# Layer 3's gate and gcn products by pairs of tiles, with seven products of half chunks

## The chip, the cores and the metric

The kernel runs on one NeuronCore of a Trainium2 chip. The metric is the device time of one execution in microseconds. Engine names are those of the profile: PE is TensorE's matmul, PEld its load of the stationary operand, DVE VectorE, ACT ScalarE, POOL GpSimd, SP SyncE. Everything is fp32.

## The reference

Four graph layers on 2708 nodes with 512 features, each behind a layernorm and a relu and added to x:

```python
h = maximum(_layernorm(x), 0.0); x = x + L0(h, adj, weight)      # relu(norm(adj + I) @ h @ W)
h = maximum(_layernorm(x), 0.0); x = x + L1(h, adj, W, b)        # norm(adj) @ h @ W.T + b
h = maximum(_layernorm(x), 0.0); x = x + L2(h, adj, W)           # relu(norm(adj + I) @ h @ W)
h = maximum(_layernorm(x), 0.0); x = x + L3(h, adj, adj, ...)
```

Layer 3, which the change is about (adj_a and adj_b are both adj):

```python
type_sum = adj @ x                                               # here x is the h above
attn_a = sigmoid(concatenate([type_sum, x], axis=1) @ Wa.T + ba)
attn_b = sigmoid(concatenate([type_sum, x], axis=1) @ Wb.T + bb)
h = x @ W_sa
scores = (h @ a_sa[0, :512])[:, None] + (h @ a_sa[0, 512:])[None, :]
e = where(adj != 0, exp(-leaky_relu(scores, 0.01)), 0.0)
x_a = (e / (sum(e, axis=1, keepdims=True) + 1e-05)) @ h
x_b = adj @ (x @ W_gcnb) + b_gcnb
return sigmoid(attn_a * x_a + attn_b * x_b)
```

The kernel forms adj @ x once and multiplies that by W_gcnb (for x_b) and by the first halves of Wa and Wb (for the two gates).

## The kernel before, in words

The nodes lie in 20 full tiles of 128 rows (tile t belongs to quarter t // 5), tile 20 with 4 x 32 rows and tile 21 with 4 x 8. `h` holds the layer's input for all tiles. `agg` holds the transposed aggregate adj @ h: its indices are the feature half f, the node half i, the chunk c of a feature half, the quarter q of a node half, and the column. A chunk is 128 features, so a tile of `agg` is four blocks of 128 x 128 (f, c), which serve as stationary operands.

`aggregate` builds `agg` by an outer scheme of seven products (numbered 1 to 7, `outer_product`), each of which runs an inner scheme of seven (`inner_x`, `inner_y`, `multiply`), for each of two column parts u. The order is 1, 7, 2, 4, the tail rows of quarters 0 and 1, 6, `ends_of_sums` (L665, L666), 5, the tail rows of quarters 2 and 3 (`tails`, L603, L608, L653), then the epilogue of tiles 0 to 9 (H1), product 3, and the epilogue of tiles 10 to 21 (H2). Products 5 and 3 write node half 1 only.

In layer 3 the epilogue is `gated`. `wg_sb` holds the gcn weights and gate columns as [128, chunk, k, 257]: 256 columns of W_gcnb and one gate column for each k. For each tile `tile_product` (L203) makes two results of 257 columns in PSUM, each the sum over four chunks; ACT takes the tanh of the last column (L1052), DVE adds the bias row (L1061), ACT multiplies by the gate (L1062), and POOL's queue stores the result to `xbs` in DRAM (L1063). Results rotate through the two banks of `ps_out`. Five more banks, `ps_agg`, serve the aggregation and the attention's `pe`.

After the epilogue the attention runs in 40 steps: `e_step` loads a block of adj and scores it on ACT and DVE (L1131, L1135, L1136), PE multiplies it by `h` (L1214) into four banks `pe0` to `pe3`, DVE sums its columns (L1225). The first step is asked for inside the last epilogue. Finished tiles go through `attention`, which loads x and xbs through `xt_places` (L916).

`ends` is a hand-laid buffer: `w_place` (the layer's weights), `misc` (four rows of 512: score vectors in layer 3's aggregation, later the column sums), `xt_places` (rows of x on the way), `y_places` (two rows) and `bg_bc` (the bias row). `take` hands out places in turn.

The program's text gives each instruction its priority and its dependences; the framework's scheduler fixes the order on each engine before the run, and may put a later instruction that it holds to be ready in front of an earlier one. Each engine then takes its own list in order.

Of the kernel before, what the change touches and what calls it, by code (L numbers as in the profile page):

```python
# [8 lines left out]
FP = mybir.dt.float32  # L9
AF = mybir.ActivationFunctionType  # L10
ALU = mybir.AluOpType

P = 128
D = 512
NC = D // P
# [3 lines left out]
KT = Q // P  # L19
# [3 lines left out]
W = (Q + 1) // U  # L23
NF = NQ * KT
# [4 lines left out]
GT = 3  # L29
# [1 line left out]


NO = 7
ENDS = NC * D + 2 * NC + (4 + GT + 1 + 2 + 1) * D


@with_exitstack
def gnn_kernel(
# [20 lines left out]
    nc = tc.nc  # L59
# [5 lines left out]
    upool = ctx.enter_context(tc.tile_pool(name="upool", bufs=1))  # L65
# [3 lines left out]
    ps_agg = ctx.enter_context(tc.tile_pool(name="ps_agg", bufs=5, space=bass.MemoryType.PSUM))  # L69
    ps_out = ctx.enter_context(tc.tile_pool(name="ps_out", bufs=2, space=bass.MemoryType.PSUM))  # L70
# [24 lines left out]
    hd = const.tile([P, NT, 4], FP, name="hd")  # L95
    mv0 = const.tile([P, NT, 2], FP, name="mv0")
    ga = const.tile([P, NT, 2], FP, name="ga")
# [5 lines left out]
    xbs = [dram.tile([P, D], FP, name=f"xbs{t}") for t in range(NT)]  # L103
# [13 lines left out]
    agg = big.tile([P, 2, 2, 2, 2, U * W], FP, name="agg")  # L117
# [4 lines left out]
    obuf = big.tile([P, NO, BLK], FP, name="obuf")  # L122
    ends = big.tile([P, ENDS], FP, name="ends")

# [12 lines left out]
    w_place, ends_o = ends[:, 0 : NC * D + 2 * NC], NC * D + 2 * NC  # L137
    misc, ends_o = ends[:, ends_o : ends_o + 4 * D], ends_o + 4 * D
    xt_places = [ends[:, ends_o + k * D : ends_o + (k + 1) * D] for k in range(GT + 1)]
    ends_o += (GT + 1) * D  # L140
    y_places = [ends[:, ends_o + k * D : ends_o + (k + 1) * D] for k in range(2)]
    ends_o += 2 * D
    bg_bc = ends[:, ends_o : ends_o + D]
    assert ends_o + D == ENDS

    def take(places):

        places.append(places.pop(0))
        return places[-1]

    def new_y():
        return take(y_places)
# [6 lines left out]
    def full_cols(a, t):  # L159
        k = t % KT  # L160
        return a[:, k * P : (k + 1) * P]

    def repeat(g, n):

        while n < P:
            nc.vector.tensor_copy(g[..., n : 2 * n], g[..., 0:n])
            n *= 2

    def tile_cols(a, t, again=False):


        cs = [a[:, f, :, c] for f in range(a.shape[1]) for c in range(a.shape[3])]
        if t < NF:
            q = t // KT
            return [full_cols(c[:, q // 2, q % 2], t) for c in cs]
        o, m = (KT * P, R0) if t == NF else (KT * P + R0 - PAD, R1P)
        if a.shape[5] == R0 + R1:
            o -= KT * P
        g = new_y().rearrange("p (c n) -> p c n", c=NC)
        for c, src in enumerate(cs):  # L180
            nc.vector.tensor_copy(
                g[:, c, 0 : NQ * m].rearrange("p (i q r) -> p i q r", i=2, q=2),
                src[:, :, :, o : o + m],
            )
        n = NQ * m
        if again:
            repeat(g[:, 0 : len(cs)], n)
            n = P
        return [g[:, c, 0:n] for c in range(len(cs))]

    def tile_product(t, cs, ws):

        n = ws[0].shape[-1]

        def bank():
            return ps_out.tile([P, n], FP, tag="out", name="po")

        po = bank()  # L200
        if t <= NF:
            for c in range(NC):
                nc.tensor.matmul(po, cs[c], ws[c], start=(c == 0), stop=(c == NC - 1))  # L203
            return po
        for c in range(NC):
            nc.tensor.matmul(po[c * G : (c + 1) * G], cs[c], ws[c], start=True, stop=True)
        y = new_y()[:, 0:n]
        nc.scalar.copy(y, po)
        po = bank()
        nc.tensor.matmul(po, all_again, y, start=True, stop=True)  # L210
        return po
# [84 lines left out]

    left = ends[:, 4 * BLK : ENDS]
    acct = [
# [734 lines left out]
    GW = D // 2 + 1  # L1033
    wg_sb = w_place.rearrange("p (c k o) -> p c k o", c=NC, k=2)
    for k in range(2):
# [5 lines left out]
            wg_sb[:, :, k, D // 2 :], wab[0:D, k : k + 1].rearrange("(c p) o -> p c o", p=P)  # L1041
        )

    def gated(ts):

        for t in ts:
            cs = tile_cols(agg, t)
            po = []
            for k in range(2):
                pk = tile_product(t, cs, [wg_sb[:, c, k, :] for c in range(NC)])  # L1050

                nc.scalar.activation(  # L1052
                    ga[:, t, k : k + 1], pk[:, D // 2 :], AF.Tanh,
                    bias=hd[:, t, 2 + k : 3 + k], scale=0.5,
                )
                po.append(pk)
            nc.vector.tensor_scalar(ga[:, t, :], ga[:, t, :], 0.5, 0.5, ALU.mult, ALU.add)
            y = new_y()
            for k in range(2):
                f = slice(k * (D // 2), (k + 1) * (D // 2))  # L1060
                nc.vector.tensor_add(y[:, f], po[k][:, 0 : D // 2], bg_bc[:, f])  # L1061
            nc.scalar.activation(y, y, AF.Copy, scale=ga[:, t, 1:2])  # L1062
            nc.gpsimd.dma_start(xbs[t], y)  # L1063

    def again(ts, fs):

# [48 lines left out]
    def column_rows(q):  # L1115

        ra, rb = (
            spool.tile([P, U * W], FP, tag=f"s{1 + k + 2 * (q % 2)}", name=f"r{k}") for k in (0, 1)
        )
        for k, r in enumerate((ra, rb)):  # L1120
            nc.vector.memset(r[:, Q : U * W], 0.0)
            nc.gpsimd.dma_start(r[:, 0:Q], ab_rows[q, k, 0:Q].partition_broadcast(P))
        return ra, rb
# [14 lines left out]
    def place(t):  # L1138

        if t < NF:  # L1140
            o = (t // KT) * Q + (t % KT) * P
            return [(0, P, o)]
        if t == NF:
            return [(q * R0, R0, q * Q + KT * P) for q in range(NQ)]
        return [(q * R1P + PAD, R1, q * Q + KT * P + R0) for q in range(NQ)]
# [25 lines left out]
    def e_step(q, u, b):  # L1171

        cu = slice(u * W, (u + 1) * W)
        ra, rb = (a[:, cu] for a in lines[q])
        if b < NQ:
            blk = load_o("y11", b, q, u)
            ts = list(range(b * KT, (b + 1) * KT))
            scores(blk, ts, ra, rb)
            return [(t, blk[:, k, :]) for k, t in enumerate(ts)], [blk]
        tl = load_tails(q, u)  # L1180
        for s in range(2):
            scores(tl[:, s : s + 1, :], [NF + s], ra, rb)
        return tl, []
# [4 lines left out]
    def gated_and_ready(ts):  # L1188

        nonlocal ready  # L1190
        if ts[0] < half:
            return gated(ts)
        gated(ts[:4])
        lines[0] = column_rows(0)
        gated(ts[4:])
        ready = e_step(*steps[0])

    hooks[6] = row_scales
    hooks[3] = lambda: again(range(half, NF), slice(0, D // 2))
    aggregate(False, gated_and_ready, hooks)  # L1200
    wsa_sb = load_w(wsa)
    todo = []
    for n, (q, u, b) in enumerate(steps):
# [35 lines left out]
        elif todo:  # L1239
            t, se_t = todo.pop(0)  # L1240
# [70 lines left out]
```

## Time and profile before

| | us |
|---|---|
| median of 3 runs | 2091.28 (2090.2 to 2091.34) |
| profiled execution | 2089.36 |
| its span, first to last instruction | 2087.6 |
| its granted TensorE clock | 0.998 of full |
| gates' products, tiles 0 to 9 | 1490.1 to 1525.2 of the span |
| gates' products, tiles 10 to 21, among attention products | 1564.8 to 1624.3 |

The span is the profile's zero to end; the time is 1.76 us longer. A row of a group names source line, engine, operation, output<-input, shapes and count; then busy time and mean duration; then the idle time of the engine before these instructions and what ended it. On PE one fp32 matmul leaves two records, and the mean duration overlaps with its neighbours', so periods are taken from the timeline.

### The profile page before, as it was taken

The numbers are of one execution on the slowest core, as the hardware profiler recorded it, in microseconds if no ns is written. First come the engines' busy times: TensorE is split into PE (matmuls) and PEld (weight loads), VectorE is DVE, ScalarE is ACT, GpSimd is POOL, SyncE is SP. The second block draws the span as 40 slices with busy tenths as digits, with TensorE's granted clock in tenths as the row PEclk, the third lists the DMA queues.
The fourth block names the chain that finished last, engine by engine and source line by source line (L and its number), as shares of the span: only waits on it lengthen the run. The fifth ranks groups of instructions, "written<-read, shape, count | busy, mean of one in ns | idle before, by whom it ended". The sixth has DMA issues, their size and how long they took to land.

```text
span 2087.6 us, 19939 instructions
## 1 busy us (share of the span) xinstructions
PE 2044.6 (98%) x7286; PEld 1272.0 (61%) x7286; DVE 1397.4 (67%) x2427; ACT 404.5 (19%) x818; POOL 193.8 (9%) x350
## 2 busy tenths in 40 slices
PE   5999999999999999999999999999999999999998
PEld 2566655656666554666664556666777666666665
DVE  4678877666767777866686889868539355565512
ACT  1430001130000011100002120000119233444411
POOL 0111111120000012100002120001001001000011
PEclk9999999999999999999999999999999999999999
DMA  9998594554545354655444564545552333233220
GB/s 370 303 378 267 184 346 166 189 191 169 173 155 190 127 181 140 239 170 172 160 155 162 201 232 169 189 154 164 179 188 74 117 104 115 98 104 102 94 71 26
DMA packets 80770, 363.65 MB, mean 174 GB/s; under 512 B 11140, under 2 KB 16172, under 8 KB 80544
## 3 DMA queue, kind: packets, MB, share of 16 engines
q1 hardware_dynamic: 50672, 245.43, 34.0%
q0 software_dynamic: 30000, 116.95, 17.3%
q8 instruction: 57, 0.93, 0.2%
q14 instruction: 41, 0.34, 0.0%
HBM read 297.38 MB, written 62.17 MB: 172 GB/s over the span
## 4 chain that ended last, share of the span: by engine, by line
PE 86%; DVE 6%; DMA 4%; issue 3%; ACT 0%; POOL 0%; SPq 0%; POOLq 0%; DVEq 0%; ACTq 0%
PE pe L1214 18%; PE po L203 15%; PE pc L541 13%; PE pa L541 13%; PE pd L541 13%; PE pb L541 7%; PE pt L603 3%; DMA obuf<-in_yb_dram 3%; PE pt L608 1%; PE pe L603 1%; DVE ends L1004 1%; DMA ends<-xs 1%; PE dg_ps L324 1%; DVE t L514 0%; DVE t L513 0%
## 5 line engine op out<-in xcount | busy, mean ns | idle before, releaser
L1214 PE MATMUL pe<-obuf,h 128*128 128x339 f32 x1280 | 372.6, 448 | 0.0
L203 PE MATMUL po<-ends,agg 128*128 128x512 f32 (+2 forms) x968 | 352.4, 521 | 2.4 <-DVE ends L1061 2.1
L1214 PEld LDWEIGHTS pe<-obuf,h 128*128 128x128 f32 x1280 | 241.3, 189 | 130.2 <-issue 12.7
L541 PE MATMUL pa<-obuf,h 128*128 128x339 f32 x1040 | 317.1, 449 | 2.5 <-ACT h L255 1.4
L203 PEld LDWEIGHTS po<-ends,agg 128*128 128x128 f32 x968 | 181.3, 190 | 156.1 <-issue 136.8
L541 PEld LDWEIGHTS pa<-obuf,h 128*128 128x128 f32 x1040 | 195.3, 189 | 109.7 <-issue 9.2
L1131 ACT ACTIVATE e<-r,nsr 128x339 f32<-128x339 f32 x352 | 171.2, 567 | 47.8 <-DVE tl L1135 15.9
L541 PE MATMUL pb<-t,s 128*128 128x339 f32 x560 | 171.3, 452 | 1.4 <-DVE t L513 0.8
L541 PE MATMUL pc<-t,h 128*128 128x339 f32 x560 | 169.4, 448 | 1.9 <-DVE u L588 1.9
L541 PE MATMUL pd<-t,s 128*128 128x339 f32 x560 | 169.0, 448 | 0.0
L541 PE MATMUL pd<-obuf,s 128*128 128x339 f32 x550 | 166.2, 448 | 0.0
L575 ACT COPY v<-pa 128x339 f32<-128x339 f32 x56 | 24.7, 440 | 723.5 <-PE pa L541 696.5
L541 PEld LDWEIGHTS pb<-t,s 128*128 128x128 f32 x560 | 106.2, 191 | 57.0 <-DVE t L513 2.1
L541 PEld LDWEIGHTS pc<-t,h 128*128 128x128 f32 x560 | 105.8, 189 | 56.9 <-DVE u L588 3.0
L541 PEld LDWEIGHTS pd<-t,s 128*128 128x128 f32 x560 | 105.9, 189 | 54.1
L541 PEld LDWEIGHTS pd<-obuf,s 128*128 128x128 f32 x550 | 104.1, 189 | 53.3 <-DVE agg L562 0.5
L541 PE MATMUL pc<-obuf,s 128*128 128x339 f32 x450 | 136.0, 448 | 0.0
L541 PEld LDWEIGHTS pc<-obuf,s 128*128 128x128 f32 x450 | 85.1, 189 | 43.8 <-issue 0.5
L935 POOL DMA_DIRECT2D xs<-ends x66 | 36.0, 545 | 782.4 <-DVE ends L934 709.9
L1231 DVE COPY agg<-pe 128x339 f32<-128x339 f32 x16 | 7.5, 507 | 150.7 <-PE pe L608 150.7
L513 DVE TENSOR_TENSOR t<-obuf,t 128x1695 f32<-128x1695 f32 x55 | 105.3, 1914 | 0.0
L514 DVE TENSOR_TENSOR t<-obuf,t 128x1695 f32<-128x1695 f32 x52 | 99.5, 1914 | 0.1
(266 smaller groups left out, 2113.5 us busy)
## 6 DMA issues: line engine op xcount, KB each, us to landing
obuf<-in_yb_dram SPq DMA_DIRECT2D x132, 847.5 KB, 4.5
obuf<-osumt SPq DMA_DIRECT2D x100, 847.5 KB, 4.5
osumt<-obuf POOLq DMA_DIRECT2D x22, 847.5 KB, 11.7
xs<-ends POOLq DMA_DIRECT2D x66, 256.0 KB, 2.3
ends<-xs POOLq DMA_DIRECT2D x61, 256.0 KB, 3.8
obuf<-in_yt_dram SPq DMA_DIRECT2D x28, 339.0 KB, 3.6
obuf<-in_yb_dram POOLq DMA_DIRECT2D x11, 847.5 KB, 11.2
ends<-in_yb_dram SPq DMA_DIRECT2D x9, 847.5 KB, 9.3
```

The costliest lines, as they stand in the source:

```text
L203: nc.tensor.matmul(po, cs[c], ws[c], start=(c == 0), stop=(c == NC - 1))
L324: nc.tensor.matmul(ps[g], first, y, start=n < 4, stop=n >= len(ops) - 4)
L513: nc.vector.tensor_add(t2, o22, t1)
L514: at_y.append(nc.vector.tensor_add(t4, o21, t2).ins)
L541: last = nc.tensor.matmul(ps, x[:, k, :], y[:, k, :], start=start and k == 0, stop=k == KT - 1, skip_group_check=not start,)
L575: at_v.append(nc.scalar.copy(v, pa).ins)
L603: nc.tensor.matmul(ps[c], h[:, NF, c * P : (c + 1) * P], tl[:, 0, :], start=start, stop=False)
L608: nc.tensor.matmul(ps[c], h[g, NF + 1, c * P : (c + 1) * P], tl[g, 1, :], start=False, stop=True)
L935: nc.gpsimd.dma_start(xs[t], xt)
L1004: nc.vector.tensor_tensor_reduce(y, h[:, t, :], vs[:, k, :], 1.0, 0.0, ALU.mult, ALU.add, hd[:, t, k : k + 1])
L1131: nc.scalar.activation(e[:, k], row, AF.Exp, bias=nsr[:, t, s : s + 1], scale=1.0)
L1214: nc.tensor.matmul(pe[c], h[:, t, c * P : (c + 1) * P], a, start=(t == 0), stop=False)
```

## The change

`gated` takes the full tiles by pairs (t, t+1). A pair's two tiles are the two rows of a 2 x 2 block matrix whose columns are the feature halves f; the weights are a 2 x 2 block matrix of feature half by k. Seven products of blocks, each two chunks deep, then give the four results. `sums_of_w` forms four sums of weight blocks once, into the space of `misc`; `sums_of_pair` forms four sums of a pair's stationary blocks, in one of two places in the space of `xt_places`; `pair_product` runs the seven parts, part p being two matmuls into pa (in `ps_out`) or pb, pc, pd (in `ps_agg`), and combines them on DVE into the rows u2 (then c12), u3 (then c21) and c22; pa becomes the first result in place. `gates` is what followed the products before. Tiles 20 and 21 go through `tile_product` as before. `ends` grows by 2 * NC = 8 floats a partition.

```diff
@@ -31,7 +31,7 @@
-ENDS = NC * D + 2 * NC + (4 + GT + 1 + 2 + 1) * D
+ENDS = NC * D + 2 * NC + (4 + GT + 1) * D + 2 * NC + (2 + 1) * D
...
+    both_places = ends[:, NC * D + 2 * NC :]
+    w_sums = both_places[:, 0 : 4 * NC // 2 * GW].rearrange("p (k c o) -> p k c o", k=4, c=NC // 2)
+    s_places = [
+        both_places[:, o : o + 4 * NC // 2 * P].rearrange("p (k c n) -> p k c n", k=4, c=NC // 2)
+        for o in (4 * NC // 2 * GW, 4 * NC // 2 * (GW + P))
+    ]
+    w11, w12, w21, w22 = (wg_sb[:, f : f + 2, k] for f in (0, 2) for k in range(2))
+    def sums_of_w():
+        t1, t2, t3, t4 = (w_sums[:, k] for k in range(4))
+        nc.vector.tensor_sub(t1, w12, w11)
+        nc.vector.tensor_sub(t2, w22, t1)
+        nc.vector.tensor_sub(t3, w22, w12)
+        nc.vector.tensor_sub(t4, w21, t2)
+    def sums_of_pair(t):
+        q = t // KT, (t + 1) // KT
+        (a11, a12), (a21, a22) = (
+            [agg[:, f, q_ // 2, :, q_ % 2, (t_ % KT) * P : (t_ % KT + 1) * P] for f in range(2)]
+            for t_, q_ in ((t, q[0]), (t + 1, q[1]))
+        )
+        sums_ = take(s_places)
+        s1, s2, s3, s4 = (sums_[:, k] for k in range(4))
+        nc.vector.tensor_sub(s3, a11, a21)
+        nc.vector.tensor_add(s1, a21, a22)
+        nc.vector.tensor_sub(s2, a22, s3)
+        nc.vector.tensor_sub(s4, a12, s2)
+        return {1: a11, 2: a12, 3: s4, 4: a22, 5: s1, 6: s2, 7: s3}
+    def pair_product(xs_):
+        ws = dict(zip((1, 2, 3, 5, 6, 7, 4), (w11, w21, w22, *(w_sums[:, k] for k in range(4)))))
+        def part(ps, k, start):
+            for c in range(2):
+                nc.tensor.matmul(
+                    ps, xs_[k][:, c], ws[k][:, c], start=start and c == 0, stop=c == 1,
+                    skip_group_check=not start,
+                )
+        def place(tag, bufs=1):
+            return upool.tile([P, W], FP, tag=tag, name=tag, bufs=bufs)[:, 0:GW]
+        pa, pb, pc, pd = (
+            (ps_out if k == 1 else ps_agg).tile(
+                [P, GW], FP, tag="out" if k == 1 else "agg", name=f"pp{k}"
+            )
+            for k in range(4)
+        )
+        part(pa, 1, True)
+        v = place("v")
+        nc.scalar.copy(v, pa)
+        part(pb, 6, True)
+        u2 = place("u2", 2)
+        nc.vector.tensor_add(u2, v, pb)
+        part(pa, 2, False)
+        part(pc, 7, True)
+        u3 = place("u3")
+        nc.vector.tensor_add(u3, u2, pc)
+        part(pd, 5, True)
+        c22 = place("s")
+        nc.vector.tensor_add(c22, u3, pd)
+        part(pc, 4, False)
+        c21 = u3
+        nc.vector.tensor_add(c21, u2, pc)
+        part(pd, 3, False)
+        c12 = u2
+        nc.vector.tensor_add(c12, u2, pd)
+        return [[pa, c12], [c21, c22]]
+    def gates(t, po):
+        for k in range(2):
+            nc.scalar.activation(
+                ga[:, t, k : k + 1], po[k][:, D // 2 :], AF.Tanh,
+                bias=hd[:, t, 2 + k : 3 + k], scale=0.5,
+            )
+        nc.vector.tensor_scalar(ga[:, t, :], ga[:, t, :], 0.5, 0.5, ALU.mult, ALU.add)
+        y = new_y()
+        for k in range(2):
+            f = slice(k * (D // 2), (k + 1) * (D // 2))
+            nc.vector.tensor_add(y[:, f], po[k][:, 0 : D // 2], bg_bc[:, f])
+        nc.scalar.activation(y, y, AF.Copy, scale=ga[:, t, 1:2])
+        nc.gpsimd.dma_start(xbs[t], y)
     def gated(ts):
+        ts = list(ts)
+        pairs = [t for t in ts if t < NF][::2]
+        xs_ = sums_of_pair(pairs[0]) if pairs else None
+        for n, t in enumerate(pairs):
+            po = pair_product(xs_)
+            if n + 1 < len(pairs):
+                xs_ = sums_of_pair(pairs[n + 1])
+            for k in range(2):
+                gates(t + k, po[k])
         for t in ts:
-            cs = tile_cols(agg, t)
-            po = []
-            for k in range(2):
-                pk = tile_product(t, cs, [wg_sb[:, c, k, :] for c in range(NC)])
-                nc.scalar.activation(
-                    ga[:, t, k : k + 1], pk[:, D // 2 :], AF.Tanh,
-                    bias=hd[:, t, 2 + k : 3 + k], scale=0.5,
-                )
-                po.append(pk)
-            nc.vector.tensor_scalar(ga[:, t, :], ga[:, t, :], 0.5, 0.5, ALU.mult, ALU.add)
-            y = new_y()
-            for k in range(2):
-                f = slice(k * (D // 2), (k + 1) * (D // 2))
-                nc.vector.tensor_add(y[:, f], po[k][:, 0 : D // 2], bg_bc[:, f])
-            nc.scalar.activation(y, y, AF.Copy, scale=ga[:, t, 1:2])
-            nc.gpsimd.dma_start(xbs[t], y)
+            if t >= NF:
+                cs = tile_cols(agg, t)
+                gates(t, [
+                    tile_product(t, cs, [wg_sb[:, c, k, :] for c in range(NC)]) for k in range(2)
+                ])
     def again(ts, fs):
@@ -1189,6 +1273,7 @@
         nonlocal ready
         if ts[0] < half:
+            sums_of_w()
             return gated(ts)
         gated(ts[:4])
         lines[0] = column_rows(0)
```

## The prediction

> **What bounds the kernel now.** I read the page first: busy shares, then the chain that ended last, then the group of the products concerned.
>
> ```profile
> PE 2044.6 (98%) x7286; PEld 1272.0 (61%) x7286; DVE 1397.4 (67%) x2427; ACT 404.5 (19%) x818; POOL 193.8 (9%) x350
> ...
> PE 86%; DVE 6%; DMA 4%; issue 3%; ACT 0%; POOL 0%; SPq 0%; POOLq 0%; DVEq 0%; ACTq 0%
> ```
>
> TensorE is busy nearly all the span and carries 86% of the chain, so TensorE time removed should reach the end, if no wait takes its place. How the waits stand must be read in the two stages that the change touches. In the groups of the window 1485 to 1640 us (busy us, mean ns | idle before) the gates' products and the VectorE work around them are
>
> ```profile
> L203 PE MATMUL po<-ends,agg 128*128 128x257 f32 x320 | 71.3, 380 | 2.1 <-DVE ends L1061 2.1
> ...
> L1061 DVE TENSOR_TENSOR ends<-po,ends 128x256 f32<-128x256 f32 x44 | 18.4, 420 | 12.2 <-ACT ga L1052 10.8 <-DMA xbs<-ends 1.4
> L1135 DVE SCALAR_TENSOR_TENSOR obuf<-obuf,e 128x1695 f32<-128x1695 f32 x8 | 15.4, 1919 | 2.5 <-ACT e L1131 2.1 <-DMA obuf<-in_yb_dram 0.3
> ```
>
> 320 records are 20 full tiles x 2 halves x 4 chunks x 2: a product leaves two records. The mean of 380 ns overlaps its neighbours; the price is the period, and stage one (tiles 0 to 9) gives it. Its timeline line, and the stage's answer of the windows view (time, then busy time of PE, PEld, DVE, ACT, POOL, clock, DMA):
>
> ```profile
> 1490.10 35.12 PE L203 MATMUL po<-ends,agg 128*128 128x257 f32 x160
> ```
>
> ```profile
> 1490.10:1524.90 34.80, 34.80 (x164) 30.09 (x161) 10.52 (x32) 11.46 (x28) 5.99 (x11) 1.00 0.30 102
> 1565.00:1625.00 60.00, 57.91 (x252) 44.30 (x251) 56.05 (x101) 50.96 (x121) 7.27 (x13) 1.00 0.23 84
> ```
>
> 80 products in about 34.8 us: **0.434 us each, without a gap**. VectorE has 24.3 us free there. The second line is stage two (tiles 10 to 21): VectorE is nearly full, because the scheduler puts the scoring of later attention steps (L1135, L1136) and column sums (L1225) into its gaps. TensorE has one real stall there:
>
> ```profile
> 1568.48 1.93 DVE L1135 SCALAR_TENSOR_TENSOR obuf<-obuf,e 128x1695 f32<-128x1695 f32 x1 [2.15 <-ACT e L1131]
> ...
> 1570.32 0.42 DVE L1061 TENSOR_TENSOR ends<-po,ends 128x256 f32<-128x256 f32 x1
> ...
> 1570.79 2.00 PE L203 MATMUL po<-ends,agg 128*128 128x257 f32 x8 [2.09 <-DVE ends L1061]
> ```
>
> A score of 1.93 us, itself late for its exponentials, stood before an eviction that TensorE needed: 2.09 us lost. This pattern decides the case.
>
> **What the Trainium skill says.** "PSUM — Partial Sum Buffer", Engine vs sequencer instructions: the queues of ScalarE and VectorE are strictly first in, first out. The three lines above agree (2.09 us). "Perfetto Trace Analysis", Optimizing Tensor Performance: independent groups of products should rotate through PSUM banks, so that evicting one overlaps the next. Stage one agrees: no gap in 34.8 us. "VectorE: DVE Perf Modes", The TRN2 errata: an fp32 tensor_tensor of N elements takes (N+151)/0.96 ns, 424 ns for 256; the trace has 420.
>
> **The change, part by part.**
>
> *Removed.* A pair of tiles took 2 x 2 x 4 = 16 products; now seven half-chunk parts of two, 14. Ten pairs (five per stage) save 20 products x 0.434 = **8.7 us**. This is the ceiling, apart from the 2.09 us stall, which might vanish as well. Tiles 20 and 21 keep their products. A part takes 0.87 us, a pair 6.07 us instead of 6.94.
>
> *Added on VectorE.* Steps between instructions queued one after another: two L1061 take 0.74 us with 0.41 each, so one of 256 or 257 columns every 0.33 us. Per pair: four sums of the stationary side and five combinations out of PSUM (u2, u3, c22, c21, c12), 9 x 0.33 = 3.0 us. With the old gate work of two tiles (four adds, two small ones, 1.5 us) that is 4.5 us per 6.07 us. Ten pairs: 30 us. Once: four sums of the weights over 514 elements, by the skill's formula 693 ns each, at most 2.8 us.
>
> *Added on ScalarE.* One copy of pa per pair; the nearest row (L208, 257 columns) is 0.376 us. Ten: 3.8 us.
>
> *Cover in stage one.* The sums of the weights read only wg_sb, loaded before the layer, and their place (misc) was last read by the h_dots near 1316 us. Tiles 0 to 9 are final once L666 has run (1444 us): products 5 and 3 write only the other node half. So these sums and the first pair's (2.8 + 1.3 us) can run in gaps like
>
> ```profile
> 1462.20 0.51 DVE L581 TENSOR_TENSOR u<-v,pb 128x339 f32<-128x339 f32 x1 [3.51 <-PE pb L541]
> 1464.99 0.93 DVE L566 TENSOR_TENSOR agg<-pa,agg 128x339 f32<-128x339 f32 x2 [2.28 <-PE pa L541]
> ```
>
> 3.51 and 2.28 us, 25 us ahead of their use. The trace shows that the scheduler does move ready work ahead: L1214 of the next stage stands among the gates. With two places for sums, those of a pair can run during the pair before. Inside a pair TensorE waits only where a bank is reused: part 4 needs u3 to have read pc, part 3 needs c22 to have read pd. Either takes 0.42 + 0.05 us, behind one part of 0.87 us. The copy v has 0.87 us before part 6 is done, and u3 has a longer lead; a 0.72 us L1062 ahead of it delays only u2. If the cover were gone, each would cost its 0.47 us, 0.9 us a pair. I take 0.4 us lost in the stage (0 to 2): gain 4.3 - 0.4 = 3.9.
>
> *Cover in stage two.* Same edits, but VectorE has no free time: 15.1 us more of its work must push scores and column sums later. Between 1630 and 1650 us it is busy 0.85 of 20 us, so 19 us stand open, and these scores are not due until their attention steps; that costs nothing. What can cost is a score just ahead of u3 or c22: 1.92 + 0.47 - 0.87 = 1.5 us. Against it stands that TensorE has ready L1214 products of 0.58 us to go on with. A check on these: pe0 to pe3 hold four of the five banks of ps_agg, and now a pair wants three, so as these products move ahead the pair's parts get fewer banks and wait more for evictions. I take one such stall beyond what before had, with small ones: 1.9 us (from -2.1, if the old stall goes too, to 8). Gain 4.3 - 1.9 = 2.4 us at this middle.
>
> *Moved.* L916 loads the attention's first x and y into xt_places; two of them ran at 1498 and 1502 us and held POOL 4.7 us. The sums of pairs now occupy the places until the last pair, near 1605 us; first use is at 1669 us, and a load lands in 3.5 us: nothing. Stores to xbs (2.3 us to land) come two at a time every 6.07 us with two places for y: free again in time. No SP transfer moves of itself. Scratch grows by 8 floats a partition: nothing.
>
> *Sum.* 8.7 - 0.4 - 1.9 = 6.4 us. The profiled execution took 2089.36 us (span 2087.6 and 1.76 around it), 1.92 below the median of 2091.28. On its scale that gives 2083.0; on the median's **2084.9 us**.
>
> **The rivals.** *Both stalls go* (faster still): if pairs keep TensorE supplied while that late score runs (five parts, 4.3 us, before u3 is needed, where two banks gave 3.5), the 2.1 us return and nothing is lost: 2091.3 - 10.8 = 2080.5. For it: the longer lead; against: u3 is still behind whatever the queue holds.
>
> *Sums in the text's order.* If the scheduler does not run them ahead, part 6 waits for c12 (0.47) and three sums (1.0) behind part 1 (0.87): 0.6 us in eight transitions, 4.8 us, and about 2.8 us at the start for the weights. 8.7 - 7.6 leaves 1.1: 2090.2. Against it: the free VectorE time and the L1214 seen ahead.
>
> *Scores in the way* (slower). In stage two each pair has three waits on VectorE (u3, c22, the next s2), 15 in all. If a score stands before one at 1.5 us, 5.8 of them eat the gain, and nine or more make it slower by over 0.2%. With two per pair: 2091.3 - 8.7 + 15 = 2097.6. For it: VectorE at 56 of 60 us, an order fixed before the run, and banks that pe takes. Against: after 1571 us the trace before shows under 0.5 us of TensorE idle from this in 50 us.
>
> *The change does not do what it says*: 14 products where 16 stood is in the loop itself, and dependent banks can't add any. Under 2%.
>
> **How the numbers follow.** About 0.2% (4.2 us) is what a measurement of this kernel can tell from no change. The main case (4.2 to 8.7 us gained) has 0.58 and, with "both stalls go" at 0.10, makes faster 0.68. Sums in order, and stage two eating most of the gain, share 0.17: within 0.2%. Scores in the way: 0.15. The range goes from 2079.5 (the ceiling of 10.8 us and 1 us of scatter) to 2092, which leaves out most of the slower case, about 0.17 in all.
>
> **What would show it.** Right: 280 records of the parts instead of 320; stage one about 31 us long with TensorE free of gaps; weight sums before 1490 us on VectorE; scores moved past 1630 us. Wrong: gaps of TensorE released by u3, c22 or the sums, repeated pair after pair; L1135 or L1136 just ahead of them; or an attention stage that begins earlier by the gain and then waits.

## The result and the profile after

| | before | after |
|---|---|---|
| median of 7 runs, us | 2091.28 (2090.2 to 2096.2) | 2082.67 (2079.3 to 2087.58) |
| profiled execution, us | 2089.36 | 2079.30 |
| its span, us | 2087.6 | 2077.5 |

The ratio is 0.9959, 95% interval 0.9945 to 0.9973: 8.6 us faster (5.6 to 11.5). A second set of runs, made beside the last experiments, gave 0.9962 (0.9949 to 0.9976).

Busy shares and the chain by engine, from the page of the changed kernel:

```profile
PE 2035.2 (98%) x7246; PEld 1264.6 (61%) x7246; DVE 1429.1 (69%) x2521; ACT 407.8 (20%) x828; POOL 193.9 (9%) x350
...
PE 81%; issue 8%; DVE 5%; DMA 5%; POOL 1%; ACT 0%; SPq 0%; POOLq 0%; DVEq 0%; ACTq 0%
```

TensorE has 40 records fewer, two for each of the 20 products removed, and VectorE 31.7 us more work. TensorE still carries most of the chain that ended last. In the groups of 1485 to 1640 us the parts of the pairs are

```profile
L1081 PE MATMUL pp<-ends 128*128 128x257 f32 x160 | 39.3, 381 | 0.0
L1081 PE MATMUL pp<-ends,agg 128*128 128x257 f32 x120 | 30.7, 382 | 1.7 <-ACT v L1097 1.7
```

280 records as forecast, and one idle time worth naming. The rest is told by five points of each PE timeline: the first gate product (where stage one, tiles 0 to 9, begins), the first matmul of product 3 (into its pa), the first gate product of stage two (tiles 10 to 21), the first tail rows of the attention's pe, and the end of the span. For the changed kernel the first four are

```profile
1488.25 1.13 PE L1081 MATMUL pp<-ends,agg 128*128 128x257 f32 x4
...
1519.21 3.02 PE L541 MATMUL pa<-obuf,h 128*128 128x339 f32 x10
...
1559.22 1.03 PE L1081 MATMUL pp<-ends,agg 128*128 128x257 f32 x4
...
1644.93 2.44 PE L603 MATMUL pe<-tl,h 128*128 128x339 f32 x8
```

Their differences, with those of the experiments for later use:

| us | stage one begins | stage one | product 3 | stage two, to the first tail rows | rest |
|---|---|---|---|---|---|
| before | 1490.10 | 34.96 | 40.02 | 89.93 | 432.59 |
| after | 1488.25 | 30.96 | 40.01 | 85.71 | 432.57 |
| pairs in stage one only | 1495.47 | 30.96 | 40.01 | 91.75 | 432.61 |
| pairs in stage two only | 1493.57 | 34.97 | 39.99 | 84.35 | 432.62 |
| sums in order | 1491.34 | 34.91 | 40.01 | 95.25 | 432.59 |
| eight parts | 1494.18 | 36.91 | 40.01 | 90.90 | 432.60 |
| sums twice | 1491.03 | 31.01 | 40.01 | 85.78 | 432.57 |
| exponentials behind v | 1491.25 | 30.96 | 40.00 | 83.26 | 432.63 |
| exponentials behind v, columns moved | 1494.27 | 30.96 | 40.00 | 82.78 | 432.59 |
| the same, again | 1491.51 | 30.96 | 40.00 | 82.65 | 432.58 |
| the change, again | 1491.47 | 30.96 | 40.00 | 87.84 | 432.63 |
| before, exponentials later | 1492.59 | 34.96 | 40.01 | 87.09 | 432.55 |

The changed kernel's span is 10.1 us shorter, but only 4.00 + 4.22 = 8.2 us lie in the two stages. The other 1.85 us lie ahead of the change, where the begin of stage one wanders over 7 us among these profiles, and over 3.2 us between the two of the change itself: scatter. Product 3 and all behind the stages keep their lengths to 0.08 us, so a stage's own time is a sharper measure than the total. It isn't free of scatter where TensorE has a gap: stage two of the change took 85.71 us in one profile and 87.84 in the other (last section).

Stages one and two after, from the windows view (the stretch, its time, busy PE, PEld, DVE, ACT, POOL, then clock and DMA), and below them stage two before:

```profile
1488.25:1519.21 30.96, 30.96 (x144) 26.36 (x141) 21.39 (x64) 11.79 (x31) 4.37 (x8) 1.00 0.26 96
1559.22:1644.93 85.71, 82.96 (x337) 60.63 (x336) 73.47 (x147) 56.58 (x132) 10.56 (x19) 1.00 0.32 111
```

```profile
1565.08:1655.01 89.93, 87.84 (x358) 64.16 (x356) 61.77 (x110) 52.65 (x124) 8.36 (x15) 1.00 0.27 94
```

In stage two TensorE idled 2.75 us after against 2.09 before. The old gap is gone and two others stand in its place:

```profile
1558.64 3.85 ACT L1215 ACTIVATE e<-r,nsr 128x339 f32<-128x339 f32 x8 [15.93 <-DMA r<-ab_rows]
...
1562.40 0.35 ACT L1097 COPY v<-pp 128x257 f32<-128x257 f32 x1
...
1562.81 1.13 PE L1081 MATMUL pp<-ends,agg 128*128 128x257 f32 x4 [1.69 <-ACT v L1097]
...
1599.24 1.92 DVE L1220 TENSOR_TENSOR obuf<-obuf,e 128x1695 f32<-128x1695 f32 x1
...
1601.07 0.62 DVE L181 COPY ends<-agg 128x128 f32<-128x128 f32 x4
...
1601.35 0.92 PE L203 MATMUL po<-ends 128*128 128x257 f32 x3 [1.06 <-DVE ends L181]
```

ScalarE's list had eight exponentials ahead of the pair's copy v. ScalarE had idled 15.93 us in front of them until their row came from DRAM. So v, whose input was done near 1560.2 us, came at 1562.4, and part 2, which adds to the bank that v reads, stood 1.69 us. Later a score (L1220) stood ahead of the copies of tile 20's columns (L181), and TensorE lost 1.06 us. VectorE has no idle time between the two: the copies began as the score ended, so there they waited for their turn and not for a store.

### The profile page after: what moved, and what is told of

Same layout as the page of the kernel before. It is cut to its first block, busy times and chain, and to the rows that moved or that the text cites. A ratio compares the mean times of both kernels' runs of the same rounds, so it can differ in the third digit from the quotient of the medians.

```text
span 2077.5 us, 19986 instructions
## 1 busy us (share of the span) xinstructions
PE 2035.2 (98%) x7246; PEld 1264.6 (61%) x7246; DVE 1429.1 (69%) x2521; ACT 407.8 (20%) x828; POOL 193.9 (9%) x350
## 4 chain that ended last, share of the span: by engine, by line
PE 81%; issue 8%; DVE 5%; DMA 5%; POOL 1%; ACT 0%; SPq 0%; POOLq 0%; DVEq 0%; ACTq 0%
PE pe L1299 17%; PE pc L541 13%; PE pa L541 13%; PE pd L541 13%; PE po L203 12%; PE pb L541 6%; DMA obuf<-in_yb_dram 3%; PE pt L603 3%; PE pe L603 1%; PE pt L608 1%; DMA osumt<-ends 1%; DVE ends L1004 1%; DMA ends<-xs 1%; PE dg_ps L324 1%; POOL xbs L1130 0%
## 5 line engine op out<-in xcount | busy, mean ns | idle before, releaser
L203 PE MATMUL po<-ends,agg 128*128 128x512 f32 (+1 forms) x648 | 281.1, 590 | 0.3 <-DVE agg L1316 0.3
L203 PEld LDWEIGHTS po<-ends,agg 128*128 128x128 f32 x648 | 121.3, 190 | 142.7 <-issue 136.5
```

## The experiments

Ratios and medians are against runs of the kernel before that were made beside each experiment. In the edits, `tc.issue_after(i)` keeps what its block writes for the engine of instruction `i` behind `i` in that engine's list.

**Pairs in one stage only**, and in the other:

```diff
-        pairs = [t for t in ts if t < NF][::2]
+        pairs = [t for t in ts if t < NF and ts[0] < half][::2]   # other run: >= half
...
-            if t >= NF:
+            if t >= NF or not pairs:
```

The other run also calls `sums_of_w` in stage two and no longer in stage one.

> Pairs for tiles 0 to 9 alone; tiles 10 to 19 go one by one as before. Theory (the gain is TensorE time removed where TensorE has no gap): stage one, from its first gate product to product 3, lasts 31.0 us as in the change (35.0 before), stage two, from its first gate product to the first tail rows of the attention, 89.9 us as before; about 4.0 us faster than before. Rival (the gain is made in stage two, where the pairs also let the old stall go): stage two carries it and this kernel gains less than 2 us. Rival (part of it comes from moved buffers: stage one begins 1.85 us earlier in the changed profile): the 1.85 us show here too, and 5.9 us in all.

> Pairs for tiles 10 to 19 alone; tiles 0 to 9 one by one. Theory: stage one 35.0 us as before, stage two 85.7 us as in the change (89.9 before), about 4.2 us faster than before. If the early start of stage one (1.85 us) came from moved buffers, it is seen here too; if it is scatter, this kernel and the first differ in it as two runs of one kernel do.

Stage one alone: 0.9980 (0.9973 to 0.9988), 2088.27 against 2092.34 us, 4.1 us. Stage two alone: 0.9964 (0.9952 to 0.9976), 2085.67 us, 6.7 us where 4.2 was expected. The stage with pairs is short and the other long, as the theory has it. Two stage times differ. Stage two without pairs took 91.75, not 89.9 us: TensorE's clock fell there (last section). With pairs alone it took 84.35, not 85.7, 5.6 us less than before: TensorE had no gap before tile 20 there. Both runs began stage one late (1495.5 and 1493.6 us), so its early start in the first profile was no part of the change.

**The sums may not run ahead.**

```diff
-            sums_of_w()
+            with tc.issue_after(at_end[-1]):
+                sums_of_w()
...
-        nc.vector.tensor_add(c12, u2, pd)
+        at_end.append(nc.vector.tensor_add(c12, u2, pd).ins)
...
-                xs_ = sums_of_pair(pairs[n + 1])
+                with tc.issue_after(at_end[-1]):
+                    xs_ = sums_of_pair(pairs[n + 1])
```

and the same around the first pair's sums (cut here).

> The change with one thing undone: the sums may not run ahead. The sums of the weights and of the first pair stand behind the last VectorE work on agg, those of each later pair behind the combination c12 of the pair before. Theory (the gain rests on the sums running in gaps): stage one waits some 3 us for the first s2 and 0.65 us at each of four transitions, 36.5 us instead of 31.0; stage two loses about 0.65 us at each transition, 2.6 us, and up to 1.9 us more where a score stands in front; 8 us slower than the change, about as before. Rival (the sums never were on the path): within 1 us of the change.

2100.36 against 2092.34 us for before, ratio 1.0035 (1.0023 to 1.0047): the change's arithmetic with this order is **slower than before**, by 8 us. About equal to before had been expected. Against the first profile of the change stage one lost 3.95 us and stage two 9.54, where 5.5 and up to 4.5 were expected. TensorE's waits of both stages (total, times, longest; L1069 makes s3, L1104 u3):

```profile
PE pp L1081 <- DVE ends L1069: 8.1, 7, 2.8
PE pp L1081 <- ACT v L1097: 4.1, 4, 2.4
PE pp L1081 <- DVE u L1104: 0.5, 1, 0.5
```

The longest, in the timeline:

```profile
1585.48 1.92 DVE L1222 TENSOR_TENSOR obuf<-obuf,e 128x1695 f32<-128x1695 f32 x1
...
1589.33 0.42 DVE L1069 TENSOR_TENSOR ends<-agg 128x256 f32<-128x256 f32 x1
...
1589.80 2.88 PE L1081 MATMUL pp<-ends 128*128 128x257 f32 x12 [2.84 <-DVE ends L1069]
```

A score delays c21 and c12, the sums stand behind those and some gate work, and part 7 waits 2.84 us for s3. Running ahead is thus worth 13.5 us in the two stages, more than the products removed; 8.1 us of TensorE's waits name s3, and v came late four times too, since the whole list had moved.

**Sixteen products again.**

```diff
         part(pa, 1, True)
+        part(pa, 1, True)
         v = place("v")
```

> The change with part 1 of every pair multiplied twice into pa (the second overwrites the first), so that a pair has sixteen products as before and all else of the change. Theory (only the number of products counts): stage one 31.0 + 5 x 0.87 = 35.3 us, stage two 85.7 + 4.3 = 90.0 us, 8.7 us slower than the change, equal to before within 1 us. Rival (VectorE is what paces the pairs, so that TensorE time is free in part): clearly less than 8.7 us slower, stage two unchanged where TensorE waits anyway.

2094.37 against 2092.34, ratio 1.0005 (0.9996 to 1.0013), equal to before within the interval. Stage one is 5.95 us longer than the change's and stage two 5.19, 4.34 of each the products. Stage one has a new wait of 1.35 us for c22 (L1108), stage two gaps of 1.82, 1.06 and 0.23 us. With as many products as before, the pairs are thus longer than the old loop in both stages, by 1.95 and 0.97 us: the gain is the number of products, no faster way of waiting.

**More VectorE work**: the four sums of a pair two or four times over.

```diff
+        for _ in range(2):                    # other run: 4
             nc.vector.tensor_sub(s3, a11, a21)
             ...
```

> The change with the four sums of each pair computed twice over (the second writes the same values), 1.34 us more VectorE time a pair: 5.8 us of VectorE for 6.07 us of TensorE. Theory (VectorE has room where it counts): stage one stays within 0.5 us of 31.0, stage two within 1.5 us of 85.7, with more scores and column sums pushed behind the pairs. Rival (VectorE is already at the edge): each pair is longer by up to 1.3 us, stage one 33 us or more, stage two 88 us or more.

> The same with the sums four times over, 4.0 us more a pair: 8.5 us of VectorE for 6.07 us of TensorE. Theory: now VectorE paces the pairs; less what runs ahead, stage one rises by up to 5 x 2.4 us, to 38 to 43 us, and stage two likewise, more where TensorE runs out of attention products. Rival (sums are always hidden): within 1 us of the change.

Twice: 31.01 and 85.78 us, nothing lost in sum (0.9958, 0.9944 to 0.9972), though here the two gaps of stage two were only 2.01 us together. Four times: 1.0038 (1.0023 to 1.0052), slower than before. The scheduler then put parts of product 3 among the first pairs, so only the sum is read: from the first gate product to the first tail rows 173.5 us, the change 156.7, that is 16.8 more, within what was expected. TensorE's two largest waits by cause are those for s3 (L1070), behind the added work, and for v (L1098):

```profile
PE pp L1082 <- DVE ends L1070: 7.6, 4, 3.0
PE pp L1082 <- ACT v L1098: 3.7, 4, 1.9
```

VectorE has room for 1.3 us more a pair and not for 4.0. The waits for s3 are under half of the 16.8 us, and some 1.7 us are a fall of TensorE's clock (last section); the rest was not taken apart.

**The gaps taken away.** First the exponentials behind v, then also the tail tiles' columns in a place for sums:

```diff
+        n = len(at_v)                          # at_v also takes the copies v of the pairs
         gated(ts[:4])
...
-        ready = e_step(*steps[0])
+        with tc.issue_after(at_v[n]):
+            ready = e_step(*steps[0])
```

```diff
-                cs = tile_cols(agg, t)
+                at = take(s_places).rearrange("p k c n -> p (k c n)")[:, 0:D]
+                cs = tile_cols(agg, t, at=at)
```

> The change with one thing moved: the exponentials of the attention's first step (L1215) may not be put ahead of the copy v of stage two's first pair on ScalarE. Theory (the 1.69 us gap of TensorE at the start of stage two is v in line behind ten exponentials that waited for their row of DRAM): that gap goes, stage two is 84.0 us, some 1.7 us less; the 1.06 us gap before tile 20 stays. Rival (the exponentials were due in time and another wait takes the place, v or u2 later, or attention products not ready): stage two stays within 0.5 us of 85.7.

> The same, and the columns of tiles 20 and 21 are copied (L181) into one of the two places for sums instead of into a row of y, so that they need not wait for the stores of the last pair. Theory: the 1.06 us gap before tile 20's products goes too, stage two 83.0 us, 2.7 us less than the change and about 11 us less than before. Rival (the copies wait for their turn on VectorE, not for the row of y): the gap stays and stage two is as in the run with the exponentials moved alone.

Exponentials behind v: 0.9943 (0.9930 to 0.9957), stage two 83.26 us, 2.45 less. The copy v now waits for its product alone, and the exponentials (eight had stood ahead of it, not ten) follow:

```profile
1563.28 0.37 ACT L1097 COPY v<-pp 128x257 f32<-128x257 f32 x1 [17.57 <-PE pp L1081]
1563.55 1.98 ACT L1215 ACTIVATE e<-r,nsr 128x339 f32<-128x339 f32 x4
```

The first gap went, and the second with it, which was not expected: the whole list had shifted. With the columns: 0.9933 (0.9919 to 0.9946), 2079.44 us, 82.78 us. As no gap was left to it, the reason given for the second gap was not tested by its going. The place does bear on the order, though: the first copies of columns stood at 1601.0 us, behind a score, without this edit, and at 1587.0 us, among the pairs, with it.

**The change once more, the old gap by itself, and the best version again**, on one chip:

> The change itself once more, beside the next two. Theory (all scatter lies ahead of stage one): stage one 31.0, product 3 40.0, stage two 85.7, the rest 432.6 us to within 0.3 us, while the begin of stage one moves by microseconds. If the gap of 1.06 us before tile 20 depends on when a store lands, it may be smaller or gone, and stage two then 84.5 us or so. Rival (the 1.85 us by which stage one began earlier belong to the change): stage one begins at 1488 us again.

> The kernel before with one thing moved: the exponentials of the attention's first step may not be put ahead of the tanh of tile 10's second half. Theory (the old 2.09 us gap has the same cause, a late score in front of the gate work, and is not tied to pairs): the gap goes, stage two 87.8 us instead of 89.9, 2.1 us faster than before, so that the pairs alone are worth 4.0 + 4.3 to 5 us against a kernel without that gap. Rival (only pairs give TensorE enough lead): the gap stays or another takes its place, stage two within 0.5 us of 89.9.

> The changed kernel with exponentials behind v and the columns of tiles 20 and 21 in a place for sums, again, now on the same chip as the change. Theory: stage two 82.8 us, 2.9 us under the change where that has both gaps; total about 2 to 3 us under it.

```diff
+        n = len(at_ga) + 1                     # kernel before; at_ga: the tanh L1052
         gated(ts[:4])
...
-        ready = e_step(*steps[0])
+        with tc.issue_after(at_ga[n]):
+            ready = e_step(*steps[0])
```

Ratios 0.9962 (0.9949 to 0.9976), 0.9987 (0.9977 to 0.9997) and 0.9950 (0.9937 to 0.9962); medians 2084.39, 2088.82 and 2079.58 against 2091.45 us. The change missed its forecast in stage two, 87.84 us for 85.7: both gaps were there, at 1.87 and 1.31 us, and the clock fell behind the first (last section). So the best version lies 4.8 us under it, more than the 2 to 3 expected. The kernel before without its gap has stage two at 87.09 us, so having the first exponentials later was worth 2.8 us there, without any pairs. This kernel and the best version in their windows:

```profile
1567.56:1654.65 87.09, 86.99 (x357) 64.47 (x356) 61.82 (x110) 53.41 (x125) 8.33 (x15) 1.00 0.28 97
```

```profile
1562.47:1645.12 82.65, 82.65 (x338) 60.37 (x337) 74.09 (x147) 57.31 (x132) 10.65 (x19) 1.00 0.34 115
```

TensorE is full in both, and they differ by 4.44 us, or 4.31 with the other profile of the best version. The ten products of a stage are 10 x 0.434 = 4.34. But the best version has the columns moved as well. The run with the exponentials alone moved, which has the same single edit as this one, took 83.26 us: 3.83 less. Tile 21's short products (L206) took 1.8 us there, 1.5 in the kernel before without its gap and 1.3 in the best version. So the products explain the gain of stage two to within half a microsecond, and some tenths either way are tile 21's.

## Why the prediction was right

*Ceiling.* 8.7 us by 20 x 0.434 us. Stage one gave 4.00, and stage two, between versions without gaps, 3.83 to 4.44. Right.

*Stage one.* Forecast 3.9 of 4.3, measured 4.00. Its 0.4 us lost was the right size: 14/16 of 34.96 is 30.59, measured 30.96. The loss is in pieces too small to be listed as waits.

*Cover.* The weight sums ran at 1315 to 1325 us, far ahead as forecast. The first pair's s3 ran at 1386 us, earlier than the forecast's 1444, since it reads only feature half 0; the other three came from 1454 us, behind L666. The run with sums in order shows that the whole gain rests on this.

*Stage two.* The mis-sized term is the 1.9 us set down for stalls beyond those of before. The gaps went from 2.09 to 2.75 us in the first profile, 0.7 us more; the gain was 4.22, not 2.4, and this is most of the difference between 6.4 and 8.2. Of 4.34 - 0.66, 0.5 us remain over; tile 21's short products (L206), 1.8 us instead of 2.1, are 0.3 of that, and the rest stays open. In the second profile, though, stage two gained only 2.09 us: gaps of 3.18 us, and 1.7 us lost to the clock, which the forecast had not in it. So the total came near the forecast although stage two lost its time elsewhere and for other reasons than forecast; that part is luck. The place was wrong as well: not u3 or c22 behind a score, but v behind exponentials on ScalarE and L181 behind a score. The forecast looked at v only behind a 0.72 us L1062 (L1129 in the changed kernel), not behind exponentials that wait for DRAM.

*Banks.* The worry that pe0 to pe3 would take the pairs' banks did not come true: TensorE ran no attention product before 1589.8 us, when the pairs were nearly done.

*VectorE's pushed work* cost nothing: VectorE is busy 17.94 of 20 us between 1620 and 1640, where before it was busy 9.85, and from 1640 to 1650 us it drops to 0.93 of 10. TensorE is full in both stretches.

*Rivals.* "Sums in the text's order" was priced 1.1 us faster than before; it is 8 us slower. Its 4.8 us for eight transitions took each sum as waiting for c12 alone. In stage two c12 itself stands behind scores: of the four waits there for the next pair's s3, three were 0.98 to 2.84 us, not 0.6, and one 0.16. With the sums on the path, "scores in the way" came true as well. "Both stalls go" did not come by itself, but with one order fixed (exponentials behind v, 83.26 us) TensorE has no gap left.

## What to carry to other kernels

An edit that trades products for sums is worth the products only if the scheduler can run the sums ahead, so count which of their inputs are final early and which places are free; here the order was worth 13.5 us and the products 8.7. When TensorE gets an added reader on another engine, read that engine's list around it, and ask what stands ahead that may wait for DRAM. Compare stages by their own length in the trace where the total scatters: in stages without gaps some tenths of a microsecond could be read here, where the totals gave 3. Profile a kernel twice where a stage has gaps: the same stage differed by 2.1 us.

## What the runs showed of the hardware

TensorE's granted clock can fall after a gap as short as 1.87 us. The change once more, whose gap ended at 1566.2 us, in TensorE's timeline and in windows of PE alone (stretch, time, busy PE, clock, DMA):

```profile
1566.20 1.42 PE L1081 MATMUL pp<-ends,agg 128*128 128x257 f32 x4 [1.87 <-ACT v L1097]
1567.41 3.35 PE L1081 MATMUL pp<-ends 128*128 128x257 f32 x8
1570.60 1.90 PE L1081 MATMUL pp<-ends,agg 128*128 128x257 f32 x8
```

```profile
1566.00:1568.00 2.00, 1.80 (x6) 0.73 0.51 204
1568.00:1570.00 2.00, 2.00 (x7) 0.50 0.00 0
1570.00:1572.00 2.00, 2.00 (x10) 0.92 0.00 0
1572.00:1580.00 8.00, 8.00 (x39) 1.00 0.18 67
```

The eight records from 1567.41 us took 3.19 us in place of 1.74, and with those before them 1.7 us went. The gaps were 0.43 us longer than in the first profile; together that is the whole of 87.84 against 85.71. The clock falls not in the gap but some 0.7 us behind its end. From the windows, 2.00 x 0.27 + 2.00 x 0.50 + 2.00 x 0.08 = 1.7 us of clock are missing, which at half rate is an estimated 3.4 us.

The run with pairs in stage one only did the same after a gap of 2.32 us (clock 0.50 from 1574 to 1576 us), which is most of its 91.75 against 89.93. So did the run with sums four times, after a gap of 2.96 us in stage one:

```profile
1520.07 4.35 PE L1082 MATMUL pp<-ends 128*128 128x257 f32 x12 [2.96 <-DVE ends L1070]
```

These twelve records took 4.35 us where twelve took 2.85 behind its second gap of 2.96 us, at 1601.1 us, after which the clock stayed at 1.00. Gaps of 1.69 (the change), 2.09 (before) and 2.84 us (sums in order) left it there too. So the length of the gap alone does not decide; what does is not shown here. The Trainium skill, "TensorE: Matmul & The Clock Gate", What's actually happening, puts the fall after at least one idle window of about 3.4 us; here shorter gaps were enough, three times in these stages, and not always. A gap of 1.87 us in a full TensorE stage thus cost nearly double, and the versions without gaps have no such fall in their stages.

Part of the scatter ahead of stage one is the same: in the profile that began it latest (pairs in stage one only, 1495.47 us) the clock was 0.50 from 274 to 278 and from 854 to 856 us, where before it was 1.00.
